# Second PSUM bank for row work, own tiles for the last group, and float16 halves for the weights of layer 2, in a four-layer graph network

## The chip, the cores and the metric

One core of one Trainium2 chip runs the whole kernel. The metric is device microseconds for one execution; lower is better. An execution is one launch: all inputs start in device memory (HBM) and the result ends there.

The core has a matrix engine (PE, TensorE), a vector engine (DVE), a scalar engine for functions and copies (ACT), a general engine (POOL, GpSimd) and a queue engine (SP). Each runs its own instructions in the order given to it and waits on semaphores for the others. PE writes only to PSUM[...], from which DVE and ACT read. Transfers are issued from the queues of SP and ACT.

## The reference

Four graph layers work on 4096 rows x of 64 numbers, with one 4096 x 4096 matrix `adj` of zeros and ones. Each layer ends with `x = layernorm(x + layer(x, adj))`. Cut to what matters:

```python
# layer 0
deg = clip(sum(adj, 1) + 1, 1)
out = relu(concat([x, (adj @ x + x) / deg]) @ W + b)
out = out / norm(out)
# layers 1 and 3 (hyperbolic attention)
adj_att = sigmoid(left[:, None] + right[None, :] + b_att) * adj
support = einsum('ij,ijd->id', adj_att, logmap(x[:, None], x[None, :]))
out = proj(expmap(x, support))
# layer 2
support = x @ weight
rank = cumsum(adj, 1); deg = rank[:, -1:]; k = min(deg, 100)
pos = rank - (deg - k)
out = (adj * where(pos > 0, 0.5 ** (k - pos), 0)) @ support + bias
```

The change touches `x @ weight` of layer 2, the ends of layers 1 and 3 (`expmap`, `proj` and the layernorm behind them, called a *move* here), and the memory that all row-wise work uses.

## The kernel before, in words

The 4096 columns of the output are cut in four *groups* of 1024 (`GROUPS`, 3 down to 0); the summed dimension is cut in 32 *blocks* of 128 (`BLOCKS`, 31 down to 0), taken two at a time as g = 15 down to 0. For every group and g, `load` (L685) brings one tile of edges of 1 MB through SP's queue; six such tiles exist. All four layers stream the whole matrix, so there are 256 loads.

*Layer 0* multiplies each edge tile with bfloat16 parts of x on PE (L1354), while DVE checks that the edges are zeros and ones (`check`, L822).

*Layers 1 and 3* run `attend` (L1011): for each block, six matmuls make the values z of 128 x 1024 pairs (L1045, L1048, L1051), ACT makes a sigmoid and a square (L1060, L1063), DVE joins them (L1066, and L1068 for two blocks at once), and two blocks later `add_up` multiplies by `xe` in float32 into one PSUM bank `acc` (L1023): two output halves of 64 columns for each block, four instructions for each g.

*Layer 2* turns the counts of edges behind a block into weights (`count` L1498, exponential in `weights_of` L1507), and adds them up with `halves` (L1511), the rows `x @ weight` split in two float16 numbers. `wide_pass` (L1441) takes groups 3 and 2 together, `narrow_pass` (L1469) groups 1 and 0 one at a time. Before it uses a block, the wide pass asks for that block's `halves`:

```python
need((2, 2 * g // WB))        # L1450
```

*Row work*, everything with one row of x at a time, is written as generators: a `yield n` asks to be called again n ticks later. They stand in two queues, and `tick` (L614) lets the head of each queue go on between the instructions of the big loops. `need(tag)` (L641) ticks until the named step is done, so that whatever is missing is put there in one piece. The row work shares one PSUM bank, `aux`: `take` (L665) hands it out and notes it in `held`, and a generator that wants it yields in `free` (L670) until `held` is empty.

The row work that matters here:

- `move` (L1084), one group's end of layers 1 and 3. Two matmuls for each half of `u` (L1102) go to `aux`, ACT copies each half (L1104), a product `x * u` (L1109) and squares follow, then some 80 operations on 128 x 8 numbers, and two big products and a sum (L1193 to L1197). For groups 3, 2 and 1 the small operations are on POOL, for the last group (0) on DVE (`Small`, L714). All groups use the same row tiles by name, each with one buffer.
- `linear` (L1200), used in layer 0 with that layer's weights and in layer 2 with `w2`: for each half of a group, four float32 transposes (L1207), a copy by ACT (L1212), four float32 matmuls (L1218), and a finishing step. For layer 2 that is `supports` (L1226): ACT rounds to float16 (L1228), DVE takes the remainder (L1229).
- `store` (L1533) issues one group's result from ACT's queue once its move is done.

In layer 1, `attention` (L1394) runs `linear` for groups 3 and 2 while later groups are still in `attend`; groups 1 and 0 fall into the wide pass of layer 2. In layer 3, groups 3 to 1 are moved while the next group is attended, and the last group's move is the end of the kernel.

The order on each engine is fixed when the kernel is built: for PE and ACT in layers 0 and 2 it is the program's own, elsewhere a scheduler sets it.

## Time and profile before

| what | value |
|---|---|
| median of 3 runs | 1134.94 us (1126.09 to 1137.0) |
| the profiled execution | 1138.77 us, its span 1137.0 us |
| PE busy | 1027.5 us, 90% of the span |
| DVE busy | 909.9 us, 80% |
| ACT busy | 802.1 us, 71% |
| POOL busy | 277.8 us, 24% |
| mean granted clock of PE | 0.951 |
| read from HBM | 269.55 MB, 238 GB/s over the span |

The profile is of one execution. Layer 0 takes the first 200 us, layer 1 the time to about 538, layer 2 to about 795, layer 3 to about 1102; after that comes the last group's move. A line number is that of the kernel before. A row of the timeline has the start, the duration, the engine, the line, the operation with its output and inputs, and how many were merged; in brackets stands how long the engine had been idle and what ended that. Busy time of PE is not PE at its peak, since matmuls are pipelined.

### The profile page before, as it was taken

The numbers are of one execution on the slowest core, as the hardware profiler recorded it, in microseconds if no ns is written. First come the engines' busy times: TensorE is split into PE (matmuls) and PEld (weight loads), VectorE is DVE, ScalarE is ACT, GpSimd is POOL, SyncE is SP. The second block draws the span as 40 slices with busy tenths as digits, with TensorE's granted clock in tenths as the row PEclk, the third lists the DMA queues.
The fourth block names the chain that finished last, engine by engine and source line by source line (L and its number), as shares of the span: only waits on it lengthen the run. The fifth ranks groups of instructions, "written<-read, shape, count | busy, mean of one in ns | idle before, by whom it ended". The sixth has DMA issues, their size and how long they took to land.

```text
span 1137.0 us, 13841 instructions
## 1 busy us (share of the span) xinstructions
PE 1027.5 (90%) x4949; PEld 406.2 (36%) x4949; DVE 909.9 (80%) x1450; ACT 802.1 (71%) x896; POOL 277.8 (24%) x649
## 2 busy tenths in 40 slices
PE   5998989789999999998989998789899999999960
PEld 2554555233333333332334323223233333333320
DVE  6577976999999999989354494544999999999964
ACT  0003122989989889986755778889899999998940
POOL 0011101010145244315400020000101444345282
PEclk9989998899999999999988999799999999999985
DMA  9999999546666566553967987478546766766300
GB/s 345 395 372 385 358 416 358 184 148 223 208 236 222 185 223 221 190 210 125 367 222 262 361 274 274 145 272 286 195 158 218 253 222 199 253 219 215 133 1 22
DMA packets 38421, 271.60 MB, mean 239 GB/s; under 512 B 4550, under 2 KB 4550, under 8 KB 5574
## 3 DMA queue, kind: packets, MB, share of 16 engines
q1 hardware_dynamic: 37440, 269.50, 65.6%
q10 hardware_dynamic: 902, 1.12, 0.3%
q8 instruction: 41, 0.67, 0.2%
q14 instruction: 38, 0.31, 0.1%
HBM read 269.55 MB, written 1.05 MB: 238 GB/s over the span
## 4 chain that ended last, share of the span: by engine, by line
PE 59%; DVE 23%; ACT 8%; POOL 4%; DMA 3%; issue 2%; ACTq 0%; SPq 0%; POOLq 0%; DVEq 0%
PE acc L1023 14%; PE z L1502 9%; DVE t L1068 7%; PE z L1045 7%; DVE t L1066 6%; PE z L1051 6%; PE z L1048 6%; PE acc L1354 6%; PE z L1514 3%; DMA edges<-in_adj_dram 3%; ACT sq L1063 3%; PE acc L1514 2%; ACT sq L1509 2%; DVE junk L824 2%; ACT sig L1060 1%
## 5 line engine op out<-in xcount | busy, mean ns | idle before, releaser
L1066 DVE SCALAR_TENSOR_TENSOR t<-z,sig 128x1024 f32<-128x1024 f32 x256 | 309.6, 1219 | 16.8 <-ACT sq L1063 10.2
L1063 ACT ACTIVATE sq<-z,turn 128x1024 f32<-128x1024 f32 x256 | 278.0, 1112 | 43.8 <-PE z L1051 18.3
L1068 DVE SCALAR_TENSOR_TENSOR t<-sq,t 128x2048 f32<-128x2048 f32 x128 | 296.5, 2316 | 0.4
L1060 ACT ACTIVATE sig<-left_b,right 128x1024 f32<-128x1024 f32 x256 | 286.0, 1147 | 3.1 <-DVE t L1066 2.7
L1023 PE MATMUL acc<-t,xe 128*64 128x512 f32 x1024 | 258.6, 612 | 16.1 <-DVE t L1068 15.9
L1045 PE MATMUL z<-edges,two_i 128*128 128x512 bf16 x512 | 201.2, 393 | 6.6 <-DVE t L1066 6.6
L1051 PE MATMUL z<-dst,src 74*128 74x512 f16 x512 | 195.4, 382 | 0.0
L1048 PE MATMUL z<-lo_hi,hi_lo 128*128 128x512 f16 x512 | 194.4, 380 | 0.0
L1509 ACT ACTIVATE sq<-z,at_edge 128x512 bf16<-128x512 f32 (+1 forms) x192 | 149.9, 829 | 49.2 <-PE z L1502 46.6
L824 DVE SCALAR_TENSOR_TENSOR t<-edges 128x2048 bf16<-128x2048 f32 x32 | 73.1, 2289 | 59.2 <-DMA edges<-in_adj_dram 59.0
L1023 PEld LDWEIGHTS acc<-t,xe 128*64 128x64 f32 x1024 | 64.2, 137 | 146.7 <-issue 86.9
L1502 PE MATMUL z<-edges,pass_by 128*128 128x512 bf16 x248 | 91.5, 409 | 19.3 <-ACT sq L1509 19.3
L1354 PE MATMUL acc<-edges,first 128*128 128x512 bf16 x256 | 84.0, 411 | 13.2 <-DMA edges<-in_adj_dram 13.1
L1045 PEld LDWEIGHTS <-two_i 128*128 128x128 bf16 x512 | 50.4, 98 | 125.8 <-issue 81.2
L1502 PE MATMUL z<-edges,enter 128*128 128x512 bf16 x256 | 92.6, 404 | 0.0
L1354 PE MATMUL acc<-edges,third 128*65 128x512 bf16 x256 | 83.0, 407 | 0.0
L824 DVE SCALAR_TENSOR_TENSOR junk<-edges 128x2048 bf16<-128x2048 f32 x32 | 73.1, 2286 | 5.3 <-DMA edges<-in_adj_dram 5.1
L1051 PEld LDWEIGHTS <-src 74*128 74x128 f16 x512 | 49.2, 96 | 70.0 <-issue 8.0
L1048 PEld LDWEIGHTS <-hi_lo 128*128 128x128 f16 x512 | 50.4, 98 | 57.5 <-issue 12.1
L1109 POOL TENSOR_TENSOR w_att<-x,u 128x512 f32<-128x512 f32 x8 | 14.4, 1798 | 183.1 <-ACT u L1104 183.1
L855 POOL TENSOR_TENSOR sq<-z 128x512 f32<-128x512 f32 x8 | 14.1, 1757 | 180.3 <-DVE z L854 159.7
L1212 ACT COPY x_t<-aux 64x512 f32<-64x512 f32 x16 | 9.2, 576 | 59.2 <-PE aux L1207 59.2
(333 smaller groups left out, 1017.5 us busy)
## 6 DMA issues: line engine op xcount, KB each, us to landing
edges<-in_adj_dram SPq DMA_DIRECT2D x256, 1024.0 KB, 5.0
x<-in_x_dram SPq DMA_DIRECT2D x4, 256.0 KB
out_dram<-x ACTq DMA_DIRECT2D x4, 256.0 KB
w_sb<-in_L_gnn_W_dram ACTq DMA_DIRECT2D x1, 32.0 KB, 4.7
given<-in_L_gnn_b_dram ACTq DMA_DIRECT2D x1, 0.2 KB
given<-in_L_gnn_bias_dram ACTq DMA_DIRECT2D x1, 0.2 KB
given<-in_L_gnn_b_att_dram ACTq DMA_DIRECT2D x1, 0.0 KB
given<-in_L_gnn_att_b_dram ACTq DMA_DIRECT2D x1, 0.0 KB
```

Of the source, the lines that this page charges most:

```text
L824: V.scalar_tensor_tensor(junk, a, 0.0, a, ALU.not_equal, ALU.not_equal, accum_out=odd[:, n : n + 1])
L1023: it = nc.tensor.matmul(acc[h * D : (h + 1) * D, :], xe[:, j, :], t[:, k, h * W : (h + 1) * W], start=j == BLOCKS[0], stop=j == BLOCKS[-1],)
L1045: nc.tensor.matmul(half, two_i, edge[:, at : at + W], start=True, stop=False)
L1048: nc.tensor.matmul(half, hi_lo[:, of], lo_hi[:, to], start=False, stop=False)
L1051: last = nc.tensor.matmul(half, src[:, of], dst[:, to], start=False, stop=True)
L1060: nc.scalar.activation(sig, left_b, AF.Sigmoid, bias=right[:, j : j + 1])
L1063: nc.scalar.activation(sq[:, k], zp, AF.Square, bias=turn, scale=-1.0 / UNIT)
L1066: V.scalar_tensor_tensor(t[:, k], zp, 0.0, sig, ALU.max, ALU.mult)
L1068: V.scalar_tensor_tensor(t, sq, HIGH**2, t, ALU.add, ALU.mult)
L1354: nc.tensor.matmul(accs[h][:m], lhs[:, j, :], edge[:, at : at + W], start=j == BLOCKS[0], stop=j == BLOCKS[-1],)
L1502: nc.tensor.matmul(z[:, h : h + W], lhs, rhs[:, h : h + W], start=j == BLOCKS[0], stop=True, skip_group_check=True,)
L1509: nc.scalar.activation(w, z[:, :n], AF.Exp, bias=at_edge, scale=-LN2)
```

## The change

Four edits:

1. *A second bank for row work* in layers 0 and 2. `take` hands out `aux` and a spare bank in turn. In layer 0 the spare is a bank of its own. In layer 2 it is the second half of a third z tile, whose first half becomes one of the wide pass's two sums; the other sum moves to the bank `acc`. Both times `spare_ends` ticks until no bank is held, and ends it. `held` still lets only one be taken at a time in the program's order.
2. *Own tiles for the last group's move*: its small numbers get names with a suffix, its big temporaries use `y` and `xw`, and in layer 3 its `u` lies in the tile `ys`. Its products with x move from POOL to DVE.
3. *Layer 2's weights by float16 halves.* `supports(s)` replaces `linear` there. ACT rounds x to float16, POOL takes the remainder, eight float16 transposes turn both halves of 128 rows at once, one ACT copy brings them back, and for each block two matmuls multiply them with the high and the low half of 512 times the weights, twice one above the other. A whole group is done at once instead of half a group.
4. For that, the weights are loaded two more times and split on DVE.

The first user of the row tile `u` in layer 0 now uses `w_att`.

```diff
@@ -662,10 +662,21 @@
 
                 return 2 + int(small * 0.33 + large)
 
+            spare, turn_of = [], [0]
+
             def take(dtype, *shape):
 
+
                 held.append(1)
-                return aux.tile(list(shape), dtype, name="aux")
+                turn_of[0] += 1
+                if not spare or turn_of[0] % 2:
+                    return aux.tile(list(shape), dtype, name="aux")
+                return spare[0](dtype, shape)
+
+            def spare_ends():
+                while held:
+                    tick(1)
+                spare.clear()
 
             def free():
                 while held:
...
@@ -1089,10 +1103,20 @@
                 least = 1e-15 if layer == 1 else 1e-30
                 at = blocks(s)
                 xg, x2g = x_of(layer)[:, at, :], x2[:, at]
+
+                last = s == GROUPS[-1]
+                G = Small(not last, "_1" if last else "")
+                E = V if last else nc.gpsimd
+                nums = G.nums
                 k, d, uu = nums("k"), nums("d"), nums("uu")
-                w, sq = grp("w_att"), grp("sq")
-
-                all_u = row.tile([P, WB, D + 1], F32, name="u_1")
+                w, sq = (grp("y"), grp("xw")) if last else (grp("w_att"), grp("sq"))
+
+                if last and layer == 3:
+
+                    all_u = ys.rearrange("p k f -> p (k f)").bitcast(F32)[:, : WB * (D + 1)]
+                    all_u = all_u.rearrange("p (k f) -> p k f", f=D + 1)
+                else:
+                    all_u = row.tile([P, WB, D + 1], F32, name="u_1")
                 u, sum_1 = all_u[:, :, :D], all_u[:, :, D]
                 for part in range(2):
                     yield from free()
@@ -1106,10 +1130,8 @@
                     )
                     held.pop()
                     yield near()
-                nc.gpsimd.tensor_mul(w, xg, u)
+                E.tensor_mul(w, xg, u)
                 nc.scalar.activation(sq, u, AF.Square)
-
-                G = Small(s != GROUPS[-1])
                 yield G.wait(0, 1) if G.on_pool else near()
                 V.tensor_reduce(uu, sq, AX.X, ALU.add)
                 yield soon()
@@ -1189,8 +1211,7 @@
                 G.stt(p, p, 1.0, r, ALU.add, ALU.mult)
                 G.mul(q, q, r)
                 yield soon()
-                E = nc.gpsimd if G.on_pool else V
-                nc.gpsimd.tensor_mul(w, xg, over(p))
+                E.tensor_mul(w, xg, over(p))
                 E.tensor_mul(u, u, over(q))
                 yield soon()
                 yield soon()
...
@@ -1223,12 +1244,37 @@
                     held.pop()
                     yield 1
 
-            def supports(at, t):
-
-                nc.scalar.activation(halves[:, at, :D], t, AF.Copy, scale=SUP)
-                V.scalar_tensor_tensor(
-                    halves[:, at, D:], t, SUP, halves[:, at, :D], ALU.mult, ALU.subtract
-                )
+            def supports(s):
+
+
+                xg = x_of(2)[:, blocks(s), :]
+                hl = row.tile([P, WB, 2 * D], F16, name="x_hl")
+                nc.scalar.copy(hl[:, :, :D], xg)
+                nc.gpsimd.tensor_sub(hl[:, :, D:], xg, hl[:, :, :D])
+                yield 2
+                yield from free()
+                t = take(F16, P, WW)
+                for k in range(WB):
+                    nc.tensor.transpose(t[:, k * P : (k + 1) * P], hl[:, k, :], ident16)
+                yield near()
+                xt = row.tile([P, W], F32, name="x_t").bitcast(F16)
+                nc.scalar.copy(xt, t)
+                held.pop()
+                yield near()
+                yield from free()
+                t = take(F32, P, WB, D)
+                for k in range(WB):
+                    for part in range(2):
+                        nc.tensor.matmul(
+                            t[:, k, :], xt[:, k * P : (k + 1) * P], w2_hl[:, part],
+                            start=part == 0, stop=part == 1,
+                        )
+                yield near()
+                at = blocks(s)
+                nc.scalar.copy(halves[:, at, :D], t)
+                V.tensor_sub(halves[:, at, D:], t, halves[:, at, :D])
+                held.pop()
+                yield 1
 
 
 
...
@@ -1248,12 +1294,20 @@
             V.memset(at_edge, -(OFF_EDGE + CUT) * LN2)
 
 
+            w2_twice = keep.tile([P, D], F32, name="w2_twice")
+            w2_hl = keep.tile([P, 2, D], F16, name="w2_hl")
+
+
             x0 = x_of(0)
             place[0] = 0
             with ExitStack() as lp:
                 own = lp.enter_context(tc.tile_pool(name="m0_own", bufs=1))
                 sb = lp.enter_context(tc.tile_pool(name="m0_sb", bufs=2))
                 ps = lp.enter_context(tc.tile_pool(name="m0_ps", bufs=6, space=PSUM))
+                rest_ps = lp.enter_context(tc.tile_pool(name="m0_aux", bufs=1, space=PSUM))
+                spare.append(
+                    lambda dtype, shape: rest_ps.tile(list(shape), dtype, name="aux_2")
+                )
 
                 first = own.tile([P, NB, 2 * D], BF16, name="first")
                 third = own.tile([P, NB, D + 1], BF16, name="third")
...
@@ -1368,6 +1422,8 @@
                             if s == GROUPS[0] and g == NB // 2 - 3:
                                 curve1, curve3, att1, att3 = constants()
                                 nc.scalar.dma_start(w2_sb, w2)
+                                nc.scalar.dma_start(w2_twice[:D], w2)
+                                nc.scalar.dma_start(w2_twice[D:], w2)
                                 later(in_turn((0, s), linear(0, s, w0_sb[:D, :], own_part)))
                             tick(4)
                         need((0, s))
...
@@ -1382,6 +1438,8 @@
                         if s > 0:
                             own_of = linear(0, s - 1, w0_sb[:D, :], own_part)
                             later(in_turn((0, s - 1), own_of))
+
+                spare_ends()
 
 
             place[0] = 1
...
@@ -1412,7 +1470,11 @@
                 anchored[0] = False
 
 
-            attention(1, curve1, (2, 1, 1, 1), lambda s: linear(2, s, w2_sb, supports))
+            V.tensor_scalar(w2_hl[:, 0], w2_twice, SUP, None, ALU.mult)
+            V.scalar_tensor_tensor(
+                w2_hl[:, 1], w2_twice, SUP, w2_hl[:, 0], ALU.mult, ALU.subtract
+            )
+            attention(1, curve1, (2, 1, 1, 1), supports)
 
 
             place[0] = 2
...
@@ -1442,8 +1504,7 @@
 
                 zs = [z_tile() for _ in two]
 
-                both = z_tile()
-                accs = [both[:, :W], both[:, W:]]
+                accs = [ps.tile([P, W], F32, name="acc"), third_z[:, :W]]
                 behind, lag = [None, None], []
                 for g in reversed(range(NB // 2)):
                     edges = [load_2(s, g) for s in two]
...
@@ -1518,7 +1579,23 @@
                             stop=j == BLOCKS[-1] and part == 1,
                         )
 
+            third_z = z_tile()
+
+            def of_third(dtype, shape):
+                t = third_z[:, W:]
+                if dtype == F16:
+                    return t.bitcast(F16)
+                n = int(np.prod(shape[1:]))
+                if len(shape) == 2:
+                    return t[:, :n]
+                names = "abc"[: len(shape) - 1]
+                return t[:, :n].rearrange(
+                    "p (%s) -> p %s" % (" ".join(names), " ".join(names)),
+                    **dict(zip(names, shape[1:])),
+                )
+
             with tc.manual_schedule(engines=FIXED):
+                spare.append(of_third)
 
                 for some in (GROUPS[:2], GROUPS[2:3], GROUPS[3:]):
                     accs = wide_pass(some) if len(some) == 2 else narrow_pass(some[0])
@@ -1526,6 +1603,7 @@
                         sums = row.tile([P, W], F32, name="sums", bufs=2)
                         nc.scalar.copy(sums, acc)
                         later(end_2(s, sums))
+                spare_ends()
 
 
             place[0] = 3
```

## The prediction

> **What bounds the kernel now.** I read the page's chain first, then the table of stretches, then the chip's timeline at the places that the change touches.
>
> ```profile
> PE 59%; DVE 23%; ACT 8%; POOL 4%; DMA 3%; issue 2%; ACTq 0%; SPq 0%; POOLq 0%; DVEq 0%
> ```
>
> The chain says TensorE, but over four layers with different limits. Rows of the table of stretches (start:end, length, then busy us and count of PE, weight loads, DVE, ACT, POOL, then granted clock, DMA share, GB/s) for layer 0, layer 1 and the join of layers 1 and 2:
>
> ```profile
> 100.00:150.00 50.00, 46.20 (x276) 26.74 (x275) 38.57 (x109) 11.93 (x19) 6.68 (x9) 0.97 0.97 385
> ...
> 350.00:400.00 50.00, 49.41 (x219) 18.31 (x217) 47.18 (x35) 43.44 (x46) 19.42 (x39) 1.00 0.59 207
> ...
> 560.00:600.00 40.00, 36.41 (x192) 15.37 (x189) 23.48 (x73) 24.56 (x29) 1.17 (x1) 0.91 0.71 261
> ```
>
> Layer 0 has its DMA at 0.97: transfers bound it. In layer 1 PE is full and DVE nearly so. Layer 2's wide pass is bound by PE (one block j takes 2.90 us, PE without a gap) until the clock falls to 0.91 around 580 us. The timeline there (start, length, engine, line, tiles, count):
>
> ```profile
> 577.24 1.05 PE L1514 MATMUL z<-sq,halves 128*64 128x512 bf16 x8
> ...
> 578.23 0.71 PE L1102 MATMUL aux<-centre,sums 128*128 128x130 f32 x4
> ...
> 579.46 0.63 PE L1207 MATMUL aux<-ident,x 128*64 128x128 f32 x4 [0.52 <-ACT u L1104]
> ...
> 581.94 1.10 PE L1218 MATMUL aux<-w_sb,x_t 64*128 64x64 f32 x8 [0.47 <-ACT u L1104]
> ...
> 582.03 1.17 POOL L1109 TENSOR_TENSOR w_att<-x,u 128x512 f32<-128x512 f32 x1 [24.75 <-ACT u L1104]
> ...
> 585.60 1.97 PE L1218 MATMUL aux<-w_sb,x_t 64*128 64x64 f32 x8 [0.67 <-ACT x_t L1212]
> ...
> 587.50 1.04 PE L1502 MATMUL z<-edges,pass_by 128*128 128x512 bf16 x2
> ...
> 592.31 0.62 PE L1502 MATMUL z<-edges,pass_by 128*128 128x512 bf16 x2
> ```
>
> The pass needs the supports of group 1 and runs all missing row steps in a row, through one PSUM bank: every step waits for the copy of the one before. PE should go on at 578.2 and does at 587.5, and then at half speed until 592.3 (1.04 for what takes 0.62). A second such burst, for group 0, ends its last block at 613.0 and goes on at 619.49.
>
> In layer 1 the same weights are applied between the attention's matmuls:
>
> ```profile
> 388.73 1.07 PE L1023 MATMUL acc<-t,xe 128*64 128x512 f32 x2
> ...
> 389.73 1.10 PE L1218 MATMUL aux<-w_sb,x_t 64*128 64x64 f32 x8
> ...
> 390.76 1.93 PE L1023 MATMUL acc<-t,xe 128*64 128x512 f32 x6
> ```
>
> Undivided, the four L1023 instructions (x8 records) take 1.94. Cut by the row work they take 3.00: the two 64-column halves no longer run side by side. So a cut costs 1.0 beside the work itself.
>
> **The change, part by part,** against the profiled execution (1138.77 us, span 1137.0).
>
> *Float16 halves, groups 3 and 2, in layer 1.* Removed for each group: two times L1207 (0.43 from start to next start at 383.05) and L1218 (1.03), and two cuts (388.73 and 395.37): 2 x 1.46 + 2 x 1.0 = 4.9 of PE. Added: 8 float16 transposes, which take 0.47 as the 8 of L929 at 682.14, and 16 float16 matmuls of 64 columns. No row has those; below, the 8 of L941 (7 columns) take 0.37, so 0.7 for 16; above, L929's 0.47 for 8 gives 0.94; I take 0.8. In the compiled order each group still cuts the four once: 0.47 + 0.8 + 1.0 = 2.3. PE saves 2.6 a group, 5.2 for both. DVE is behind it: five intervals of L1023 from 384.24 to 413.24 took 29.0 against 23.1 undisturbed, with some 2 us of row work on DVE, so PE stays last after the change; z buffers and ACT (+0.3 a group) will keep some of it back. I take 4.5, bounds 1.5 and 5.2.
>
> *First burst (group 1).* Now: ACT is free of its exponentials at 578.62; the float16 copy takes 0.62 (row of `ys`, 128x512); POOL subtracts; PE transposes 0.47; ACT copies 128x1024 in 1.01 (row of L933); PE multiplies 0.8; then the pass goes on. The two products for u use both banks and fit under POOL's subtraction, as do their copies. For POOL the nearest row is L1109's 1.17 above, in the same burst with an idle DVE; its other executions average 1.80. The Trainium skill (GPSIMD Engine Reference, section 4.1 Engine selection) speaks against this step: elementwise work on two inputs belongs on VectorE, GPSIMD being about twice as slow. Twice DVE's 0.69 (row L901) is 1.38. By the row the sum is 578.62 + 0.62 + 1.17 + 0.47 + 1.01 + 0.8 = 582.7, with four hand-overs of about 0.15 some 583.3; by the rule 583.5. Against 587.5 that saves 4.2 or 4.0. A rule on the clock (TensorE: Matmul & The Clock Gate, What's actually happening) says an idle window of about 3.4 us halves the clock and a busy one restores it. The row shows half speed for 6.7 us (585.6 to 592.3), about two such windows. Were the new stall under 3.4, the half speed would go, and 1.9 more (4.8 for what takes 2.9); at 5 us it stays, and some new matmuls meet it (0.8 becomes 1.3). I take 3.7, bounds 2.5 and 6.
>
> *Second burst (group 0).* In the old kernel its first transposes already ran inside the pass (0.45, no wait); now the whole chain stands behind the exponentials: 612.8 + 0.62 + 1.17 + 0.47 + 1.01 + 0.8, hand-overs and half speed 1.1, gives 618.0 against 619.49. Saved 1.4, bounds 0 and 3. Group 0's x must be there: last group's row chain ended at 605.76 and starts no later now.
>
> *Own tiles for the last group.* The tail seems to ask for it:
>
> ```profile
> 1102.83 1.23 PE L1102 MATMUL aux<-centre,sums 128*128 128x130 f32 x4 [0.68 <-ACT sums L1074]
> ...
> 1111.87 0.34 ACTq L1534 DMA_DIRECT2D out_dram<-x  x1
> ...
> 1112.25 0.38 ACT L1104 COPY u<-aux 128x260 f32<-128x260 f32 x1 [9.47 <-POOL x L1197]
> ```
>
> ACT copies u 8 us after PE made it, when POOL has let go of the old u. But between them stands the store of group 1, issued from ACT's own queue, and it waits for the same POOL sum (1110.66 to 1111.84). In the changed kernel's order that store still stands ahead of the copies and still waits for POOL. So the copies stay at 1112.25. What is left: x*u on DVE (0.69) for POOL's 1.17, but in line with two reductions, 0.4; at the end two products of 0.69 on DVE for one beside POOL's 1.56, 0.3. I take 0.7, bounds 0 and 1.
>
> *Second bank.* In layer 0 and in layer 2's narrow passes the steps are ticks apart, and each is copied out long before the next. Layer 0's waits of PE on that bank sum to some 8 us, all under a DMA at 0.97: nothing, at most 2. In the bursts it is counted above. Its price: the sums of the wide pass now share the bank of layer 1's last sum, so the first add-up waits for that copy (0.59, 0.7 with the hand-over), and the pass's two z buffers are the last ones freed. Against this DVE's last pair step and its order around the first check change by up to 2.3. I take 0.5 saved, bounds 1.5 on both sides.
>
> *Two more weight loads.* Issued on ACT behind w2, whose load took 7.6 us beside the edges. DVE waits for both at about 15.3; queued behind are the first two checks, which free edge buffers, and PE's constants. Two more small transfers may hold DVE 1.5 us longer, at most as much DMA gap. I take 0.5 lost, bounds 0 and 1.5. Two DVE products of 128x64 (0.2 each) lie in a stretch with DVE at 3.9 of 5 us: nothing.
>
> Sum: 4.5 + 3.7 + 1.4 + 0.7 + 0.5 - 0.5 = 10.3 of 1138.77, or 0.90%. The median of the runs shown is 1134.94, 3.8 below the profiled execution; the same share gives 1124.7.
>
> **Rivals.** *DVE takes over in layer 1* and the bursts keep their half speed for longer: 1.5 + 2.5 + 0.5 + 0.5, about 5, so 1130. For it: DVE at 47.18 of 50 there. Against: PE has no gap in the cut intervals, DVE has.
>
> *The own tiles free the tail:* copies at 1104.1 instead of 1112.25; DVE's conversion for group 1 at 1104.6 lies just ahead, the rest moves by 8. Sum 18, so 1117. Against it stands the store; only if ACT's queue didn't wait for a store's source could it be.
>
> *The subtraction on POOL stops PE,* the slower side. PE's transposes wait in order behind it. POOL's 0.20 operations took 2.32 where DVE's long pass ran (L745 at 514.93). If each subtraction takes 1.8 and such a wait of 2.3, and PE has no room before it, layer 1 loses 4.1 twice and half speed for a window pair (3.3 twice), the bursts 2.9 each: 20.6 lost, less the 10.3, so 10 slower, 1145. It decides when the subtraction lands more than 2.6 us after PE arrives in layer 1. Against: between copy and transposes stand at least 9 attention matmuls and four add-ups, some 4 us.
>
> **Numbers.** About 1% is what a measurement of this kernel tells from no change. Main case 0.56, at 1120 to 1130, a little over half of it beyond 1% (under 1123.6); DVE takes over 0.28; tail free 0.08; POOL stops PE 0.08. Faster 0.38, same 0.54, slower 0.08. The range runs from 1115 to 1136: from the tail case to the bounds of the second case with half a per cent for the runs.
>
> **What would show it.** Layer 1's add-ups at 4.6 us intervals with one of about 7 for each group, not two; PE back in the wide pass some 5 us after it stops, in both bursts, with matmuls at half rate behind; the last u copies still straight after the store of group 1; POOL subtractions of 1.0 to 1.4. Wrong it would be if copies precede the store, if PE shows waits on the new tile in layer 1, or if the join of layers 1 and 2 moves by more than 2.

## The result and the profile after

The changed kernel takes 1116.54 us (median of 1114.64 to 1117.97); the kernel before, run beside it, 1130.51 (1125.21 to 1137.0). The ratio is 0.9847, with an interval from 0.9813 to 0.9881: 1.5% faster, which is 17 us by the ratio (the two medians, of four executions each, differ by 14.0), where 0.9% and 10 us were forecast. The profiled execution took 1117.97 us (span 1116.2), 20.8 less than the profiled one of before.

The chain of work that ended last hardly differs from the one before (PE 58% for 59%, DVE 22% for 23%, ACT 9% for 8%). The table of stretches, for layer 1 and for the join of layers 1 and 2 (busy us and count of PE, weight loads, DVE, ACT, POOL, then granted clock, DMA share, GB/s):

```profile
350.00:400.00 50.00, 49.14 (x230) 17.89 (x233) 48.30 (x35) 46.18 (x48) 22.40 (x43) 1.00 0.59 202
560.00:600.00 40.00, 34.87 (x218) 14.02 (x219) 29.16 (x95) 28.52 (x32) 2.83 (x2) 1.00 0.82 312
```

Layer 1 still has PE full, with DVE a little fuller. In the second line the clock is 1.00 where it was 0.91: that is the first of the surprises. The timeline of the first burst of row work in the wide pass, TensorE alone:

```profile
568.86 0.60 PE L1575 MATMUL z<-sq,halves 128*64 128x512 bf16 x4
569.39 0.71 PE L1126 MATMUL aux<-centre,sums 128*128 128x130 f32 x4
569.94 0.61 PE L1126 MATMUL z<-centre,sums 128*128 128x130 f32 x4
571.58 0.62 PE L1258 MATMUL aux<-ident,x_hl 128*128 128x128 f16 x8 [1.03 <-POOL x_hl L1253]
573.30 0.64 PE L1268 MATMUL z<-w_hl,x_t 128*128 128x64 f16 x16 [1.10 <-ACT x_t L1261]
574.01 0.39 PE L1563 MATMUL z<-edges,pass_by 128*128 128x512 bf16 x1
574.24 0.61 PE L1563 MATMUL z<-edges,enter 128*128 128x512 bf16 x2
```

PE leaves the pass at 569.39 and is back at 574.01, after 4.6 us for 9.3, and the matmuls behind run at 0.61, full speed. The second burst still stops longer, and half speed (1.05) follows:

```profile
599.65 0.62 PE L1258 MATMUL aux<-ident,x_hl 128*128 128x128 f16 x8 [2.64 <-POOL x_hl L1253]
601.38 0.64 PE L1268 MATMUL z<-w_hl,x_t 128*128 128x64 f16 x16 [1.10 <-ACT x_t L1261]
602.24 0.63 PE L1563 MATMUL z<-edges,pass_by 128*128 128x512 bf16 x1 [0.22 <-issue]
602.67 1.05 PE L1563 MATMUL z<-edges,enter 128*128 128x512 bf16 x2
```

In layer 1 each group cuts the four attention instructions once:

```profile
385.55 1.93 PE L1037 MATMUL acc<-t,xe 128*64 128x512 f32 x6
387.41 0.64 PE L1268 MATMUL aux<-w_hl,x_t 128*128 128x64 f16 x16
387.99 1.07 PE L1037 MATMUL acc<-t,xe 128*64 128x512 f32 x2
```

And at the end, the store of group 1 and the last group's copies of u:

```profile
1092.12 0.34 ACTq L1612 DMA_DIRECT2D out_dram<-x  x1
1092.50 0.38 ACT L1128 COPY ys<-aux 128x260 f32<-128x260 f32 x1 [8.88 <-POOL x L1218]
```

The copies still follow the store.

**Where the time went, by stage.** A stage runs from the start of one of DVE's instructions to the start of another; these all stand in the trace: layer 1's first *pair step* (the one that joins two blocks, L1068 before, L1082 after), its last, the first check of edges in the narrow passes (L824, L838), layer 3's first pair step, its last, and DVE's last instruction. us, profiled executions; "again" is the first experiment, the others single parts of the change:

| | before | again | bank alone | own tiles alone | halves alone | after |
|---|---|---|---|---|---|---|
| up to layer 1 | 208.2 | 205.5 | 200.0 | 206.1 | 205.1 | 205.2 |
| layer 1 | 323.4 | 323.5 | 323.3 | 323.5 | 317.8 | 317.6 |
| join and wide pass | 106.4 | 106.6 | 102.0 | 106.8 | 95.8 | 97.8 |
| narrow passes | 149.2 | 149.2 | 147.3 | 145.7 | 148.3 | 146.5 |
| layer 3 | 309.9 | 309.9 | 307.8 | 309.8 | 309.8 | 310.1 |
| tail | 34.4 | 34.4 | 34.4 | 33.6 | 34.4 | 33.7 |

Between before and its repeat every stage but the first agrees within 0.3. So layer 0 carries the chance, and the profiled execution of before was 2.7 us slow there. Against the repeat, 18.6 us went: 5.9 in layer 1, 8.8 in the join and the wide pass, 2.7 in the narrow passes, 0.7 in the tail, 0.3 up to layer 1 and 0.4 behind DVE's last instruction; layer 3 took 0.2 more.

### The profile page after: what moved, and what is told of

Its sections match the earlier page's. It is cut to its first block, busy times and chain, and to the rows that moved or that the text cites. A ratio compares the mean times of both kernels' runs of the same rounds, so it can differ in the third digit from the quotient of the medians.

```text
span 1116.2 us, 13744 instructions
## 1 busy us (share of the span) xinstructions
PE 996.4 (89%) x4861; PEld 393.9 (35%) x4949; DVE 912.1 (82%) x1452; ACT 803.4 (72%) x892; POOL 271.0 (24%) x649
## 3 DMA queue, kind: packets, MB, share of 16 engines
HBM read 269.58 MB, written 1.05 MB: 242 GB/s over the span
## 4 chain that ended last, share of the span: by engine, by line
PE 58%; DVE 22%; ACT 9%; POOL 4%; DMA 4%; issue 3%; ACTq 0%; SPq 0%; POOLq 0%; DVEq 0%
PE acc L1037 14%; PE z L1563 9%; DVE t L1082 8%; DVE t L1080 6%; PE z L1062 6%; PE acc L1408 6%; PE z L1059 6%; PE z L1065 6%; PE acc L1575 3%; DMA edges<-in_adj_dram 3%; ACT sq L1077 3%; ACT sq L1570 3%; ACT sig L1074 2%; PE z L1575 1%; PE aux L943 1%
## 5 line engine op out<-in xcount | busy, mean ns | idle before, releaser
L1080 DVE SCALAR_TENSOR_TENSOR t<-z,sig 128x1024 f32<-128x1024 f32 x256 | 308.9, 1218 | 13.8 <-ACT sq L1077 7.7
L1082 DVE SCALAR_TENSOR_TENSOR t<-sq,t 128x2048 f32<-128x2048 f32 x128 | 297.4, 2323 | 0.5
L1037 PE MATMUL acc<-t,xe 128*64 128x512 f32 x1024 | 255.6, 611 | 18.4 <-DVE t L1082 17.9
L1059 PE MATMUL z<-edges,two_i 128*128 128x512 bf16 x462 | 181.5, 393 | 8.1 <-DVE t L1080 8.1
L838 DVE SCALAR_TENSOR_TENSOR t<-edges 128x2048 bf16<-128x2048 f32 x32 | 73.0, 2288 | 52.8 <-DMA edges<-in_adj_dram 52.8
L1563 PE MATMUL z<-edges,pass_by 128*128 128x512 bf16 x241 | 87.6, 400 | 18.4 <-ACT sq L1570 17.6
L1408 PE MATMUL acc<-edges,first 128*128 128x512 bf16 x241 | 78.0, 400 | 16.1 <-DMA edges<-in_adj_dram 15.5
L1563 PE MATMUL z<-edges,enter 128*128 128x512 bf16 x240 | 85.0, 397 | 0.5
L838 DVE SCALAR_TENSOR_TENSOR junk<-edges 128x2048 bf16<-128x2048 f32 x32 | 73.1, 2286 | 4.6 <-DMA edges<-in_adj_dram 4.3
L1575 PE MATMUL acc<-sq,halves 128*64 128x512 bf16 x384 | 61.6, 398 | 2.6 <-issue 1.6
```

The costliest lines, as they stand in the source:

```text
L838: V.scalar_tensor_tensor(junk, a, 0.0, a, ALU.not_equal, ALU.not_equal, accum_out=odd[:, n : n + 1])
L1037: it = nc.tensor.matmul(acc[h * D : (h + 1) * D, :], xe[:, j, :], t[:, k, h * W : (h + 1) * W], start=j == BLOCKS[0], stop=j == BLOCKS[-1],)
L1059: nc.tensor.matmul(half, two_i, edge[:, at : at + W], start=True, stop=False)
L1080: V.scalar_tensor_tensor(t[:, k], zp, 0.0, sig, ALU.max, ALU.mult)
L1082: V.scalar_tensor_tensor(t, sq, HIGH**2, t, ALU.add, ALU.mult)
L1408: nc.tensor.matmul(accs[h][:m], lhs[:, j, :], edge[:, at : at + W], start=j == BLOCKS[0], stop=j == BLOCKS[-1],)
```

## The experiments

**The kernel before again.**

> The kernel before once more, unchanged. It asks how much of the 20.8 us between the two profiled executions (1138.77 and 1117.97) is chance. Theory A (chance): the profiled execution of before was a slow one, its excess lies in layer 0, which waits for transfers; this profile reaches layer 1's first add-up some 3 to 6 us earlier than 208.23 and ends near 1130. Theory B (the change acts in layer 0): layer 1 begins within 1 us of 208.23 again. Ratio 1.000 either way.

1134.24 us, ratio 0.9997 (0.9975 to 1.0019). Layer 1's first pair step came at 205.51, not 208.23. That is nearer to Theory A, 2.7 us for its 3 to 6; but the profiled execution took 1136.58 us and did not end near 1130. Of the 20.8 us, some 2 to 3 are chance.

**One part at a time.** The bank alone is the change's `take`, the spare tiles of layers 0 and 2 and the new `accs`:

```diff
-                return aux.tile(list(shape), dtype, name="aux")
...
+                if not spare or turn_of[0] % 2:
+                    return aux.tile(list(shape), dtype, name="aux")
+                return spare[0](dtype, shape)
...
-                accs = [both[:, :W], both[:, W:]]
+                accs = [ps.tile([P, W], F32, name="acc"), third_z[:, :W]]
```

> Only the second bank (layers 0 and 2), on the kernel before. Theory A: layer 0 gains nothing beyond chance; in the wide pass's bursts the float32 row work of group 1 alternates over two banks, so two of its copies overlap the next step, 1 to 2 us a burst, and the narrow passes do not move; time 2 us less, ratio 0.998. Theory B: the bank is what brings layer 0's 5 us and the narrow passes' 2.5 us; then about 8 us less, ratio 0.993.

1121.90 us, ratio 0.9898 (0.9870 to 0.9926): 11.5 us, far more than the prediction (0.5) or Theory A (2) and more than Theory B (8). By stages against the repeat: 5.5 up to layer 1, 4.6 in the join and the wide pass, 1.9 in the narrow passes, 2.1 in layer 3. Of the 4.6, 3.6 lie in the first burst, which no half speed follows here.

The own tiles alone:

```diff
-                w, sq = grp("w_att"), grp("sq")
+                w, sq = (grp("y"), grp("xw")) if last else (grp("w_att"), grp("sq"))
...
-                nc.gpsimd.tensor_mul(w, xg, u)
+                E.tensor_mul(w, xg, u)
```

> Only the own tiles of the last group, on the kernel before. Theory A (the store in front of the copies still holds them): the tail from the last add-up on shortens by 1.0 us, the copies still start right behind the store of group 1, nothing else moves; ratio 0.999. Rival (own tiles free the row chains of the last group in layers 1 to 2 too, and with it the narrow passes): 3 us or more less, and the pass over group 2 in layer 2 shorter by 2.

1132.97 us, ratio 1.0017 (0.9996 to 1.0037): no change to be told. The tail is 0.7 shorter and the copies still wait, as Theory A has it. The profile also shows the narrow passes 3.5 shorter, which looks like the rival, but the median of the times does not follow; the reason comes below.

The float16 halves alone, through one bank:

```diff
-            attention(1, curve1, (2, 1, 1, 1), lambda s: linear(2, s, w2_sb, supports))
+            attention(1, curve1, (2, 1, 1, 1), supports)
```

> Only the float16 halves for layer 2's weights, with one bank, on the kernel before (and the scratch tile of the first parts renamed, for room). Theory A: layer 1 saves 5.2 us as in the whole change (2.6 a group); the first burst saves some 5 of its 6.7, since one bank makes the last group's second product wait for the copy of its first (0.5 to 1.0), the second burst its whole 1.7; in all 12 us, ratio 0.989. Rival (the two banks are what removes the half speed in the first burst): the burst saves 3 and matmuls after it run at half speed (1.04 for 0.62); in all 9 us, ratio 0.992.

1120.95 us, ratio 0.9905 (0.9870 to 0.9941). The ratio lies between the two theories. Layer 1 saves 5.7 (5.2 expected). Join and wide pass save 10.8, more than in the whole change: the join is 1.8 shorter than with the bank, the first burst keeps one stretch of half speed (1.04 for 0.62, as the rival said, from 571.80 to about 575), the second burst has none. Here is that second burst, on TensorE:

```profile
599.48 0.62 PE L1237 MATMUL aux<-ident,x_hl 128*128 128x128 f16 x8 [2.54 <-POOL x_hl L1232]
601.21 0.64 PE L1247 MATMUL aux<-w_hl,x_t 128*128 128x64 f16 x16 [1.10 <-ACT x_t L1240]
601.68 0.62 PE L1537 MATMUL z<-edges,pass_by 128*128 128x512 bf16 x2
602.14 0.61 PE L1537 MATMUL z<-edges,enter 128*128 128x512 bf16 x2
```

The waits, 2.54 and 1.10, are nearly those of the changed kernel above, 2.64 and 1.10. There the clock halved, here it did not.

**The store that stands ahead.** The changed kernel with

```diff
-                nc.scalar.dma_start(out[:, blocks(s), :], x_of(4)[:, blocks(s), :])
+                (nc.sync if s == 1 else nc.scalar).dma_start(
+                    out[:, blocks(s), :], x_of(4)[:, blocks(s), :]
+                )
```

> The changed kernel with the store of group 1 issued from the queue of SyncE, not of ScalarE. Theory A (the store was what held the last u copies): they start about 0.6 us after the products, some 8.2 us before the end of group 1's move, and the whole tail moves up: 8 us less than the changed kernel, ratio to before about 0.978. Rival (the copies, or the last group's work on VectorE, wait for GpSimd's chain of group 1 through something else, such as the conversions on VectorE at 1084.8): 0 to 3 us less.

1103.40 us, ratio 0.9712 (0.9671 to 0.9752). The tail fell from 33.7 to 26.4, 7.3 for the 8.2 expected. The times fell by more, 13.1 between the medians; in the profile, 2.2 of it lie in layer 3 and 1.8 ahead of layer 1, where the edit changes nothing. The timeline of the tail:

```profile
1078.80 0.38 ACT L1128 COPY ys<-aux 128x260 f32<-128x260 f32 x1 [0.80 <-PE aux L1126]
...
1085.23 0.92 DVE L759 TENSOR_TENSOR rs_t<-r_t 128x8 f32<-128x8 f32 x1
1086.19 0.97 DVE L739 SCALAR_TENSOR_TENSOR rs_t<-rs_t,t 128x8 f32<-128x8 f32 x1
...
1088.43 0.35 SPq L1612 DMA_DIRECT2D out_dram<-x  x1
```

The copy starts 9.6 us ahead of the store instead of behind it. Counted from the last pair step it also comes 9.6 us earlier than in the changed kernel (5.7 for 15.3). Not all of that is kept: three of DVE's small steps took 0.92 to 1.04 for 0.17, 2.4 us more in all, while GpSimd did its last three long products for group 1 (1085.09 to 1088.40).

**The subtraction on VectorE.**

```diff
-                nc.gpsimd.tensor_sub(hl[:, :, D:], xg, hl[:, :, :D])
+                V.tensor_sub(hl[:, :, D:], xg, hl[:, :, :D])
```

> The changed kernel with the subtraction of the halves on VectorE in place of GpSimd. Theory A: the bursts gain 0.5 (first: 0.69 for 1.16) and 0.3 (second: the subtraction waits on VectorE for a check that ends at 598.5), layer 1 loses 0.7 twice since VectorE has no room there (4.67 us of work in a period of 4.67); sum 0.6 slower, no change in time. Rival (the rule that such work belongs on VectorE): 0.5 to 1 us gained in each burst, no loss in layer 1, 2 us less.

1114.86 us, ratio 0.9809 (0.9766 to 0.9852), not told apart from the changed kernel's 0.9847. The subtraction took 0.69 for 1.16, and the first burst gained 0.5. Two blocks later PE waited for an exponential (0.62) and a block took 0.8 more. Layer 1 took 317.6, as in the changed kernel. So the profile shows neither the loss of Theory A nor the rival's 2 us; the intervals of the times are too wide to tell 2 us.

**Halves made as soon as x is there.** `split` does the copy and the subtraction, on the engine `E`.

```diff
+                if layer == 1:
+                    made[s] = split(E, s)
```

> The changed kernel with both halves of x made as soon as a group's x is there (copy and subtraction on GpSimd for groups 3 to 1, on VectorE for group 0), not when the wide pass needs them. Theory A: the first burst loses its wait of 1.03, the second its wait of 2.64 and with that its half speed (1.4), ScalarE saves 0.6 in each: 5 us less than the changed kernel. Rival (the half speed is set by the whole burst and not by the long wait): the second burst keeps half speed for 3 us, 3.5 us less in all.

1110.63 us, ratio 0.9778 (0.9734 to 0.9821). The wide pass is 5.2 shorter, 0.7 in the first burst and 4.3 in the second, which keeps full speed: Theory A. Layer 1 lost 0.7 and the narrow passes 1.7, so up to layer 3 its profile keeps 2.8, not 5.

**The first burst made longer.**

```diff
-                nc.gpsimd.tensor_sub(hl[:, :, D:], xg, hl[:, :, :D])
+                for _ in range(3 if s == 1 else 1):
+                    nc.gpsimd.tensor_sub(hl[:, :, D:], xg, hl[:, :, :D])
```

> The changed kernel with GpSimd's subtraction for group 1 done three times over, so that TensorE's wait in the first burst grows from 1.03 to about 3.3 us (4 with slow subtractions). Theory A (a wait of TensorE of some 2.6 to 3.4 us halves the clock): matmuls after it take 1.04 for 0.62 for some 3 us, and the pass loses 2.3 for the wait and 1.4 or more for the clock, 3.7 us in all. Rival (the clock did not matter in the first burst): 2.3 us lost, matmuls at 0.62 at once.

1123.36 us, ratio 0.9882 (0.9833 to 0.9931). TensorE in that burst:

```profile
575.54 0.78 PE L1259 MATMUL aux<-ident,x_hl 128*128 128x128 f16 x8 [3.83 <-POOL x_hl L1254]
577.42 1.04 PE L1269 MATMUL z<-w_hl,x_t 128*128 128x64 f16 x16 [1.10 <-ACT x_t L1262]
...
579.11 1.05 PE L1564 MATMUL z<-edges,enter 128*128 128x512 bf16 x2
```

The wait grew by 2.8 (3.83 for 1.03), the burst cost 5.4 more; the other 2.6 go with the half speed that came with the wait. Theory A: the half speed was a real part of what the change had removed.

**The bank in layer 0 alone.** The spare tile is there for layer 0 only, on the kernel before.

> Only the second bank, and only in layer 0, on the kernel before. The bank alone gave 11.5 us, of which its trace shows 3.6 in the first burst, 0.7 in the second and some 2 in the narrow passes; layer 1's first pair step stood 5.5 us earlier than in the repeat of before (200.00 against 205.51). Theory A (the bank shortens layer 0): 4 to 6 us less than before, ratio 0.996, first pair step of layer 1 near 200. Rival (that profile's layer 0 was chance): ratio 1.000, first pair step at 204 to 208.

1129.66 us beside 1135.92, ratio 0.9942 (0.9923 to 0.9961): 6.3 us, Theory A by the times. Its profiled execution, at 1135.1 the slowest of this kernel, has the first pair step at 204.68, where the rival put it. This step moves by chance: over all 18 profiles it stands at 205.1 to 210.4 without the bank in layer 0 (five, mean 207.1) and at 200.0 to 209.2 with it (thirteen, mean 203.8). What the second bank can save there shows in the repeat of before, where PE waits five times until VectorE has read the one bank (L1317), 0.73 to 0.83 us each; one of them:

```profile
149.49 0.61 PE L929 MATMUL aux<-ident,ys 128*74 128x128 f16 x8 [0.83 <-DVE z L1317]
```

**The extra weight loads later.** The two loads of `w2_twice` are issued at the end of layer 0's second group.

> The changed kernel with the two extra loads of layer 2's weights issued at the end of layer 0's second group, not at its start. Theory A (the loads make VectorE wait at the start, first check at 18.6 for 14.7, and eat what the bank gives in layer 0): first check at about 14.5, layer 0 shorter by 3 to 5, time 4 us less than the changed kernel. Rival (the transfers of layer 0 take the delay back by its end anyway): start earlier by 4 and time within 1 us of the changed kernel.

1115.66 us, ratio 0.9825 (0.9806 to 0.9844): no gain to be told. VectorE starts its checks at 14.57, 4 us earlier, as expected, but then, in group 2:

```profile
101.78 0.20 DVE L1474 TENSOR_SCALAR w_hl<-w_twice 128x64 f16<-128x64 f32 x1 [6.59 <-DMA w_twice<-in_L_gnn_weight_dram]
...
102.48 2.28 DVE L838 SCALAR_TENSOR_TENSOR junk<-edges 128x2048 bf16<-128x2048 f32 x1
```

The compiled order puts the conversion of the weights right behind their load, wherever that is. In the changed kernel the same wait of 6.04 stands at 18.24. The wait was moved, not removed; the rival's outcome, by another road.

**Both gains, and the loads.** The store moved and the halves early; then with the loads late:

> The changed kernel with the store of group 1 on the queue of SyncE and the halves of x made as soon as x is there. Theory A (the two gains lie at different places and add up): 7.3 from the tail and 5.2 from the bursts, 12.5 less than the changed kernel, ratio to before about 0.973 by traces. Rival (they share something): 9 us or less.

> The same with the extra weight loads issued late as well. Theory A: 16 us less than the changed kernel, about 1100. Rival (layer 0 takes the delay back anyway): as without the late loads, 12.5 less.

1103.78 us, ratio 0.9721 (0.9698 to 0.9743), and 1105.12, ratio 0.9740 (0.9714 to 0.9766). The rivals: no better than the store alone. In the profiles the wide pass keeps its 5.0 and the tail its 7.3; 1.4 goes back in the narrow passes and 0.5 in layer 1. Of the 2.7 left between its profile and that of the store alone the times show nothing.

**Weights first.** The three loads are issued behind those of layer 0's weights.

> The changed kernel with all three loads of layer 2's weights issued among the first of the kernel, ahead of the attention vectors. Theory A (VectorE's wait of 6.0 us for the extra weights holds two checks back, these the edge buffers, and that costs layer 0 some 4 us): first check at 14 to 15 for 18.6, no later wait for the weights, 4 us less than the changed kernel, ratio to it 0.997. Rival (layer 0's transfers take it back): within 1 us.

1112.82 us, ratio 0.9813 (0.9793 to 0.9833); the changed kernel's is 0.9847, its interval from 0.9813. The first check came at 17.52, not 14 to 15, and VectorE still waited 5.79 for the weights, at 14.45: the expected mechanism was not produced. Inconclusive.

**The change without its own tiles, and without layer 0's bank.**

> The changed kernel without the own tiles of the last group (second bank and float16 halves kept). Theory A (own tiles shorten the narrow passes by 3 and the tail by 0.7, as the profile of them alone shows): narrow passes 149 for 146.4, tail 34.4 for 33.7, 3 to 4 us more than the changed kernel. Rival (the bank shortens the narrow passes, the profile of the own tiles alone was chance): tail 0.7 longer, nothing else.

> The changed kernel without the second bank in layer 0. Theory A (the bank gives layer 0 some 6 us in the times): 4 to 6 us more than the changed kernel, ratio to before near 0.989. Rival (behind the wait for the weights the bank gives nothing): within 1 us of the changed kernel.

Without own tiles: 1115.95 us, ratio 0.9833 (0.9816 to 0.9850), as the whole change. The tail is 0.7 longer and the narrow passes take 145.0, not 149: the rival. Own tiles gave 0.7 us in the tail, and nothing else that repeats. Without layer 0's bank: 1120.61, ratio 0.9871 (0.9852 to 0.9891), 4.7 more than the kernel without own tiles beside it, and the first pair step at 210.43 for 201.77. Against the changed kernel itself it is 2.7 by the ratios, whose intervals overlap. Theory A, with less certainty than on the kernel before: in the whole change the bank in layer 0 is worth some 3 to 5 us.

**All that seemed to help.**

> The store of group 1 on SyncE's queue, the halves of x made early, and the loads of layer 2's weights issued first. Theory A: 3 to 4 us less than with the store and the early halves alone, ratio to before near 0.968. Rival: as those two alone, 0.972.

1103.28 us, ratio 0.9715 (0.9696 to 0.9734): the rival again. Moving the store alone gives the same within the intervals, and it is a change of one line.

**The clock, counted.** The trace records the clock that was granted to TensorE. In all 18 profiled executions it is 1.0 or 0.5, every stretch between two changes is a whole multiple of 3.413 us, and within an execution all changes fall on one grid. One step of that grid is called a *window* here. The table of stretches of before shows it over the first burst (third number from the end is the clock):

```profile
581.60:585.00 3.40, 1.73 (x12) 1.32 (x12) 1.75 (x4) 1.33 (x4) 1.17 (x1) 0.98 0.00 0
585.00:588.40 3.40, 2.80 (x11) 2.13 (x12) 1.93 (x12) 0.93 (x2) 0.00 (x0) 0.50 0.02 5
588.40:591.80 3.40, 3.40 (x13) 1.06 (x13) 2.82 (x22) 1.88 (x3) 0.00 (x0) 0.52 0.66 205
```

and of the changed kernel:

```profile
569.30:572.70 3.40, 1.87 (x18) 1.42 (x16) 1.71 (x3) 2.74 (x6) 1.16 (x1) 1.00 0.43 181
572.70:576.10 3.40, 2.73 (x27) 1.41 (x30) 1.96 (x8) 2.35 (x4) 0.00 (x0) 1.00 0.28 43
```

One window at half speed costs at most 1.7 us, half of 3.413, and less where PE waits anyway. Windows at half speed, counted by stage:

| | before | again | bank alone | own tiles alone | halves alone | after | store moved |
|---|---|---|---|---|---|---|---|
| wide pass | 4 | 4 | 2 | 4 | 1 | 1 | 1 |
| narrow passes | 6 | 6 | 3 | 2 | 5 | 4 | 4 |
| layer 3, first quarter | 1 | 1 | 0 | 1 | 1 | 2 | 0 |

This accounts for most of the odd rows of the table of stages. The narrow passes follow the count in all 18 profiles but one. Measured from their first exponential to layer 3's first pair step, they take 141.0 to 141.1 us with six windows (three profiles), 139.8 to 140.4 with five (six), 138.7 to 138.8 with four (seven) and 137.9 with two; the bank alone is out of line, 139.6 with three. From two to six windows that is 0.8 us for each.

In layer 3, thirteen profiles have the same order of work, and in each PE waits 2.35 to 2.39 us at the same place for a step of DVE (L1080 in the changed kernel). Eleven of them have no window at half speed and take 307.8 to 307.9 us; the kernel with the late loads has one and takes 308.8, the changed kernel has two and takes 310.1. (Before and the other four, among them its repeat, have another order there, always one window, and take 309.8 to 309.9.) The changed kernel and the one with the store moved, each in the window that ends the wait and in the next:

```profile
796.46:799.87 3.41, 1.70 (x8) 0.60 (x7) 3.41 (x17) 2.35 (x4) 2.17 (x7) 1.00 0.36 72
799.87:803.28 3.41, 2.76 (x13) 1.54 (x13) 3.41 (x5) 2.48 (x4) 0.02 (x1) 0.50 0.56 235
```

```profile
794.50:797.91 3.41, 1.83 (x8) 0.60 (x7) 3.41 (x19) 2.35 (x4) 2.03 (x7) 1.00 0.29 53
797.91:801.32 3.41, 2.19 (x19) 1.25 (x19) 3.41 (x5) 3.10 (x5) 0.15 (x1) 1.00 0.61 255
```

The waits are equal, 2.35 and 2.36, but the grid lies 0.13 us differently against them. So PE is busy 1.70 us of one window and 1.83 of the other, and only the first is followed by half speed. In the narrow pass over group 2, too, PE waits 1.88 us for an exponential before and 1.75 after, for the same row work on ACT. Before, PE is busy 45% of that window, and half speed follows and costs 1.5 us; after, 64%, and none follows.

A count over the 18 traces, from 210 to 1060 us, has 4335 windows at full clock. PE was busy under 45% in 81 of them, and half speed followed 80; with 45 to 53% it followed 13 of 27; above that, 5 of 4227, all five in the second burst of kernels with the old float32 row work. So half speed goes with the work of PE in a whole window, with a limit near one half, and not with the length of one wait. The limit is rough, since the profile models the ends of matmuls.

The time follows the clock outside the profiles as well. Of 76 executions of the kernel before, measured beside the experiments, the shortest took 1125.0 us at a mean clock of 0.965 and the longest 1139.6 at 0.949; the correlation of time and clock is -0.92.

## Why the prediction was wrong

Its direction held, and so did most of its mechanisms; the sum was 7 us short, and 1116.54 lies below the main case of 1120 to 1130. By the profiles, the change against the repeat is 18.6 us for a forecast of 10.3. Of the 8.3 between them, 3.2 lie in the join and the wide pass, nearly all in the first burst, 2.7 in the narrow passes, 1.4 in layer 1 and 0.8 ahead of layer 1. The steps, in its order:

- *Float16 halves in layer 1: 4.5 (1.5 to 5.2).* Measured 5.7 to 5.9, in the change and with the halves alone. The sixteen float16 matmuls took 0.58 from start to next start, below the lower bound of 0.7; each group cut the four once. Nothing was kept back by DVE, for which 0.7 had been taken off.
- *First burst: 3.7 (2.5 to 6).* **This step failed.** From the add-up at 577.24 before, two blocks took 13.79 + 3.19 us for a regular 5.80, so 11.2 were lost; after, 7.28 + 2.90, so 4.4. Saved 6.8. The stall itself came out as added up, 4.6 from stop to return for the forecast 5.1 (578.2 to 583.3). What failed is "at 5 us it stays", said of the half speed: the stall is two waits of 1.03 and 1.10 with work between, the emptiest window of the grid has PE busy 54% (49% before), and no window was at half speed. The prediction priced that case, at 1.9 more, and turned it down by the length of the whole stall.
- *Second burst: 1.4 (0 to 3).* From 8.2 to 6.5, so 1.7; the half speed stayed, as forecast.
- *Own tiles: 0.7 (0 to 1).* Measured 0.7, and the store held the copies, as the experiment with the store shows. The rival that gave 1117 has nearly the measured time, but its mechanism did not occur; that the range, drawn down to 1115 for it, holds the measured time is luck.
- *Second bank, in layer 0 "nothing, at most 2".* **This step failed.** Layer 0's bank is worth 6.3 us on the old kernel and some 3 to 5 on the new one. A stage with its DMA at 0.97 was taken as bound by transfers alone, but PE's waits within it count, and "each is copied out long before the next" does not hold there. In the repeat of before, PE waits 4.0 us in five pieces for VectorE's division of the sums (L1317), the last reader of the one bank; one of the five is shown with the experiment. With two banks (the bank alone) these are gone and 2.4 stand behind another step. How 1.6 to 4 us of waits become 3 to 6 of time is not shown. The clock may have a part in it: ahead of layer 1 the profiles without this bank have 8.4 windows at half speed on average, those with it 6.7.
- *Second bank, in the join of layers 1 and 2: 0.5 saved (1.5 on both sides).* From the last pair step to the second add-up of the wide pass it is 7.95 us for 8.01, so 0.1. The halves alone take 6.1: in the join the bank costs 1.8, where the prediction put 0.7.
- *The narrow passes: nothing.* They are 2.7 shorter, with four windows at half speed for six; measured from the first exponential, 2.3 us lie between profiles with six and with four. The clock was not in the sum. The bank is not needed for it, since the own tiles alone, with one bank, have two windows and 145.7 us.
- *Weight loads: 0.5 lost (0 to 1.5).* **Mis-sized:** VectorE waits 6.0 us for them, and its first check comes 3.2 us later than in before's profile, 4.0 later than in the repeat. What that costs in time is not shown. The bank's gain lies in the same layer, and up to layer 1 the changed kernel shows no more than 0.3 against the repeat; that the two cancel is argued, since neither experiment that moved the loads freed VectorE of its wait.
- *DVE takes over* did not happen: with another 0.7 us for each group on DVE, layer 1 still took 317.6. *POOL stops PE* did not either: the two subtractions in the wide pass took 1.16 and, beside a DVE check, 1.67.

The Trainium skill's rule on elementwise work (GPSIMD Engine Reference, section 4.1 Engine selection; 0.69 on VectorE for 1.16 on GpSimd) held for the instruction; in the kernel's time no gain could be told (1114.86 us and 1116.54). Of its rule on the clock (TensorE: Matmul & The Clock Gate, What's actually happening) the prediction used the length, 3.4 us of idleness. Measured here, a window need not be idle: one with PE busy 49% was followed by half speed. The same section says that the window is free-running, and that is the half that mattered: the grid of 3.413 us is in every trace here.

What stays open: the limit between 45% and 53%. The halves alone kept full clock after two windows with PE busy just under 45% and 48%, around the waits of 2.54 and 1.10, while the changed kernel, with 2.64 and 1.10, had one of 33% there and lost it. Open, too, is why the old second burst fell with 53% to 68%. The place of a wait against the grid can't be set, so it was not tried as an experiment; the pair of layer 3 came by chance.

## What to carry to other kernels

Cut a stall of TensorE into short waits with matmuls between, so that TensorE works for well over half of each window, or take it out, and count the windows at half speed beside the stall: here they were some 2 of the 7 us of one burst, and most of the gain of the narrow passes, which looked like that of the bank or of the own tiles. Small effects of under 4 us in one profiled stage may be such windows, so set the stage beside its clock before crediting an edit. And look for what a queue holds behind a waiting instruction: the best gain on top of the change, 7.3 us of the tail, was one store moved to another queue.

## What was not expected of the hardware

The granted clock changes only on a grid of 3.413 us, and equal waits of 2.35 us are followed by half speed in two traces and not in eleven, by their place on it. Two loads of 16 KB issued beside full edge transfers took 8.2 us (median) to land, and the first instruction that uses them makes VectorE's whole queue wait 6.0 us. Three of VectorE's small steps of 0.17 us took 0.92 to 1.04 while GpSimd ran its products of 128x512.
